# A fused decoder layer on one core: row maxima of two head groups turned over in one tile, the last decision tree finished by halves, and a new planned order

## The chip, the cores and the metric

The kernel runs on one core of a Trainium2 chip. The metric is the device time of one execution in microseconds. Three runs of the kernel before gave 995.1, 996.6 and 993.88 us; their median, 995.1 us, is the time before. In the text, PE is the matrix engine (TensorE), ACT the activation engine (ScalarE), DVE the vector engine (VectorE), POOL is GpSimd, and SP issues the DMAs.

## The reference, cut to what matters

The input is x of shape (2, 1024, 256): 2048 tokens of 256 features, and a context of 2 x 77 rows. Three residual blocks follow each other.

```python
# 1: causal self attention, 16 heads of 16 features, then an iterated cell and a feed-forward layer
xn = ln(x, g_attn, b_attn); q, k, v = split(xn @ qkv_w + qkv_b)
w = softmax(where(causal, -inf, q @ k.T / 4)); attn = (w @ v) @ out_w + out_b
x = x + attn; xs = ln(x, g1, b1); vs = 0
for _ in range(8):
    u = tanh(attn @ w_ctx + xs @ w_x + b_inl)
    vs = vs + 0.1 * (u - xs - vs); xs = xs + 0.1 * vs
x = x + xs; h = ln(x, g2, b2); x = x + gelu(h @ ff_w1 + ff_b1) @ ff_w2 + ff_b2
# 2: cross attention to the 77 context rows, 16 heads, same softmax
# 3: eight decision trees of 255 nodes each
logits = x @ W_in.T + b_in                   # (2048, 8 * 255)
reached = the 8 nodes per tree on the path that the signs of the logits choose
out = (silu(logits) * reached) @ W_out.T
```

Each block's input is first normalised, and its output is added to x.

## The kernel before, in words

The 2048 tokens are cut into NTB = 4 blocks of TB = 512; blocks 0 and 1 are the first sequence, 2 and 3 the second (BPB = 2 blocks a sequence). All arithmetic is fp32 except for small bf16 constants. An fp32 matmul of the program appears in the profile as two PE instructions; a transpose of a 128 x 128 piece as one. The 16 heads lie in NG = 4 groups of 4; a head has a slot of SLOT = 32 partitions, of which the odd ones hold its 16 features and the even ones are free, so the four heads of a group multiply at once on four 32-row strips of the array.

For each block six kinds of stages exist:

- `scores(tb)`: norm, then `queries` (for block 0 `first_queries`): projections of q and k, moved by DMA into the slot layout `qT`, `kT`, values into `v`; then for every group g `maxima(tb, g, q)`: scores with the queries on the partitions, a DVE `tensor_reduce` per head that writes the negated row maximum into the tile `nm`, and `shift`.
- `values(tb)` (`weights` and `weighted`): for each group, once `(tb, g)` is in `done`: scores again with the keys on the partitions, ACT's exponential into `p`, POOL's `affine_select` for the causal mask, the products with `v` (128 x 32 column strips), and `weigh`, which divides by the sum.
- `opening(tb)`, `middle(tb)`: output projection; the cell (`liquid`, eight dependent steps, products with `w_dx`), the feed-forward layer, and `cross_attention`, whose inner function `tops` calls `cross_maxima(xq, k, g)` for the groups one after the other.
- `leaves(tb)` (`trees`): per tree t two halves of 128 nodes: product with the first weights, ACT's bias and halving (`th`), DVE's comparison (`td`), ACT's tanh (`ta`), a DVE product that makes the silu, one product of the signs with the path matrix per half, and a DVE comparison that keeps the reached nodes. The products with the second weights are taken for two trees at a time, for each of DC = 2 output halves `oc` (`outwards`).

How the row maximum gets into the softmax is what the change is about. In `shift(q, nm)` (L814) PE transposes the four 128 x 128 pieces of `nm` into one PSUM bank, and DVE adds the bank to the group's queries. In `nm` only the first column of each slot is written, the others are zero, so after the transpose only partition 0 of each slot carries a value; the keys' partition 0 of each slot is 1 (from `_key_bias`, and the vector `shift`), so the second score product subtracts the maximum by itself. Three tiles `nmax0..2` go round in the list `spare`; each is held from the first reduce of a group to its transposes.

The order on every engine is written out by the program as it builds. `Clock` keeps an account of when each engine is free and each piece of a tile is written and read (`pieces` says at what fineness), with a cost for every operation; `weave` (L380) always takes the next step that can start first by this account, a tie going to the stage whose place in `PLACES` comes first, and `PATIENCE` says for how long a stage is passed over for one that would not make PE wait. So a changed cost, place or patience changes the order of the queues of all engines; what is computed stays. [...]

Of the kernel before, what the change touches and what calls it, by code (L numbers as in the profile page):

```python
# [40 lines left out]
for _name, _k in (  # L41
    ("g_attn", 2), ("b_attn", 2), ("bq", 2), ("bk", 2), ("out_b", 2), ("g1", 2), ("b1", 2),
    ("b_inl", 2), ("g2", 2), ("b2", 2), ("ff_b1", 8), ("xbq", 2), ("xbk", 4),
    ("b_in", 2 * PAR), ("rights", 2), ("shift", 1), ("sbq", 4), ("sbk", 4),
):
    _COLS[_name] = (_n, _k)
    _n += _k
# [12 lines left out]


PLACES = {
    "middle": ((-26, 208), (261, 484), (534, 668), (797, 996)),
    "leaves": ((320, 619), (567, 756), (824, 1044), (1188, 1260)),
    "scores": ((-300, -80), (-51, 138), (138, 375), (464, 619)),
    "opening": ((-24, 87), (181, 344), (399, 404), (656, 885)),
    "values": ((-257, -85), (-141, 85), (251, 381), (434, 634)),
}
PATIENCE = {
    "prepare": 0.5, "projections": 0.3,  # L70
    "middle": 0, "leaves": 0.26, "scores": 0.09, "opening": 0.33, "values": 0,
}


# [32 lines left out]
class Clock:  # L107
# [4 lines left out]
    HANDOVER = 0.06  # L112
    MARGIN = 0.72
    TURNS = {FULL: 0.2, ROWS: 0.215, COLUMNS: 0.135}
    ALONE, MIXED = 1.11, 0.14
    WINDOW, WARM = 3.413, 0.38
    SETS = {AF.Gelu: "gelu", AF.Exp: "exp"}

    def __init__(self, nc):
        self.nc = nc  # L120
        self.pe = 0.0
        self.dma = 2.2
        self.at = {"act": 0.0, "dve": 0.0, "pool": 0.0, "dma": 0.8}
        self.written = {}
        self.used = {}
        self.banks = [0.0] * 8
        self.table = None
        self.mode = (P, P)
        self.each = 0.0
        self.children = []  # L130
        self.window, self.done, self.speed = 0, 0.0, 0.5

    @staticmethod
    def pieces(ap):

        if not hasattr(ap, "ap"):
            ap = ap[:]
        dims = ap.ap
        starts, width = [ap.offset % (dims[0][0] or 1 << 30)], 0
        for step, n in dims[1:]:  # L140
            if step >= P:
                starts = [at + step * i for at in starts for i in range(n)]
            else:
                width += step * (n - 1)
        return {(ap.name, i) for at in starts for i in range(at // P, (at + width) // P + 1)}

    def ready(self, aps):
        return max((self.written.get(p, 0.0) for ap in aps for p in self.pieces(ap)), default=0.0)
# [85 lines left out]
        )  # L234

    def pool(self, name, out, *args, **kw):
        cost = 0.15 + out.free_size() * (0.0009 if name == "affine_select" else 0.0021)
        cost += 0.82 if ALU.pow in args else 0.0

        def issue():  # L240
            if name == "affine_select":
                self.nc.gpsimd.affine_select(out=out, in_=args[0], **kw)  # L242
            else:
                getattr(self.nc.gpsimd, name)(out, *args, **kw)

        return Op("pool", cost, 0.06, out, args, issue)
# [198 lines left out]
def decoder_kernel(ctx: ExitStack, tc: tile.TileContext, ins: dict, out: bass.AP):  # L445
# [19 lines left out]
    def bank():  # L465
        return banks(1)[0]
# [68 lines left out]
    def col(name, i):  # L535
        at = _COLS[name][0] + i
        return vecs[:, at : at + 1]
# [73 lines left out]
    def fill_late():  # L611
        for t in (qT[1], xq, *nmax[2:]):
            yield zeros(t)
        for g in range(NG):
            src = col("shift", 0).to_broadcast([P, S - TB])
# [198 lines left out]
    def shift(q, nm):  # L814


        yield (nm,), 1
        pt = bank()
        for qi in range(NQ):
            clock.transpose(pt[:, qi * P : (qi + 1) * P], nm[:, qi, :], ident)  # L820
        spare.append(nm)
        yield clock.vector("tensor_tensor", q, q, pt, ALU.add)
        clock.free(pt)


# [13 lines left out]
    def queries(tb, xn):  # L839
# [10 lines left out]
            cols = slice(i * P, (i + 1) * P)  # L850
            yield from project_values(v[:, first + i], xn[:, :, cols], wv, vrow[:, 0, :], P, f"v{tb}_{i}")
        done.add((tb, "projected"))
        for g in range(NG):
            yield from maxima(tb, g, q)
            done.add((tb, g))

    def first_queries(xn):

# [10 lines left out]
            done.add((0, "projected"))  # L869

        clock.spawn(others(), PATIENCE["projections"])
        for g in range(NG):
            yield (), lambda: len(made) > g and all(m() for m in made[g])
            yield from maxima(0, g, q)
            done.add((0, g))

    def weights(tb):

# [8 lines left out]
        yield from features_first(aT, at, f"a{tb}")  # L887
        done.add((tb, "aT"))

    def maxima(tb, g, qT):  # L890

        blk = tb % BPB
        yield (), lambda: bool(spare)
        nm = spare.pop(0)
        slots = nm.rearrange("p i (j s) -> p i j s", s=SLOT)[:, :, :, 0]
# [48 lines left out]
        yield from shift(qT[:, g, :], nm)  # L944

    def cross_maxima(xq, k, g):
        yield (), lambda: bool(spare)
        nm = spare.pop(0)
        slots = nm.rearrange("p i (j s) -> p i j s", s=SLOT)[:, :, :, 0]

        def one(j, ps, qi):
            r = slice(j * SLOT, (j + 1) * SLOT)
# [14 lines left out]
        yield from shift(xq[:, g, :], nm)  # L967

    def weighted(tb, g, qT, at):

# [182 lines left out]
    def cross_attention(tb, x):  # L1153
# [4 lines left out]
        ready = []  # L1158

        def tops():  # L1160
            for g in range(NG):
                yield from cross_maxima(xq, k, g)
                ready.append(g)

        clock.spawn(tops())
        at = dtile(f"xat{tb}", (P, NQ, D))
# [41 lines left out]
    def trees(tb):  # L1208
# [12 lines left out]
        def outwards():  # L1221
# [10 lines left out]
            ]  # L1232
            yield (), lambda: all(m() for m in made)
            for t in range(0, PAR, 2):
                yield (), lambda: len(acts) > t + 1
                w2 = [outof[tb * PAR + t + n] for n in range(2)]
                made = []
                for oc in range(DC):
                    for n in range(2):
                        for i in range(2):  # L1240
                            act = acts[t + n][:, i, :]
                            yield (act, w2[n]), 1 if n == i == 0 else None
                            if n == i == 0:
                                ps = bank()
                            clock.matmul(
                                ps, w2[n][:, i, oc * P : (oc + 1) * P], act,
                                start=n == i == 0, stop=n == i == 1,
                            )
                    at = y[:, oc, :]
                    op = clock.vector("tensor_tensor", at, at, ps, ALU.add)  # L1250
                    made.append(clock.beside(added(op, ps, oc, t + 2 == PAR)))
# [7 lines left out]
        for t in range(PAR):  # L1259
# [5 lines left out]
            )  # L1265
            dec = work.tile([P, TB], BF16, tag="dec", name=f"td{tb}_{t}", bufs=2)

            for i in range(2):
                for c in range(DC):
                    yield (xn, w1), 1 if c == 0 else None  # L1270
# [8 lines left out]
                clock.free(ps)  # L1279
                if i == 0:  # L1280
                    yield clock.vector("tensor_scalar", dec, h[:, 0, :], 0.0, None, ALU.is_gt)
            into.more()
            yield clock.activation(act, h, AF.Tanh)
            yield clock.vector("scalar_tensor_tensor", act, act, 1.0, h, ALU.add, ALU.mult)


            for i in range(2):
                yield (dec,), 1
                ps = bank()
                clock.matmul(ps, paths[:, i, :], dec, start=True, stop=True)  # L1290
                yield clock.vector(
                    "scalar_tensor_tensor", act[:, i, :], ps, col("rights", i), act[:, i, :],
                    ALU.is_equal, ALU.mult,
                )
                clock.free(ps)
            acts.append(act)
        yield (), lambda: (tb, "trees") in done


# [121 lines left out]

def _key_bias(v):

    out = _slots(v, 1).reshape(H, SLOT)
    out[:, 0] = 1.0
    return out.reshape(-1)


# [25 lines left out]
def _arrays(a):  # L1454
# [7 lines left out]
    shift = np.tile(np.arange(SLOT) == 0, P // SLOT).astype(np.float32)  # L1462
# [45 lines left out]
```

## Time and profile before

| What | Value |
|---|---|
| runs | 993.88, 995.1, 996.6 us (median 995.1) |
| profiled execution | 993.91 us, its span 992.2 us |
| clock granted to PE | 1.000 of full |
| PE busy | 944.4 us (95%), 6256 matrix instructions |
| DVE busy | 622.3 us (63%), 1357 instructions |
| ACT busy | 411.4 us (41%) |
| POOL busy | 84.6 us (9%) |
| DMA | 44.97 MB, mean 45 GB/s |

A row of a group says: source line, engine, operation, written tile<-read tiles, shapes, count | total busy us, mean ns of one | idle time of that engine just before, and what ended it. The mean ns of a PE instruction is its latency through the pipe; the next one may start earlier, so costs on PE are read here from the distance of starts. `nmax` is the tile `nm` of the code, `bank` any of the eight PSUM banks; L182 is the line that issues every matmul, L198 every transpose, L233 every DVE and L223 every ACT operation.

### The profile page before, as it was taken

What the parts mean: (1) busy time and instruction counts of PE and PEld (TensorE: products, weight loads), DVE (VectorE), ACT (ScalarE), POOL (GpSimd) and SP (SyncE); (2) the same over time, 40 slices, a digit from 0 to 9 for tenths busy, and PEclk for the clock granted to TensorE, in tenths of its full rate; (3) what the DMA queues carried; (4) which work ended last, traced back from release to release, by engine and by line L of the source; (5) the groups of instructions that cost most, each with busy time, mean ns of one, the idle gap of its engine ahead of it and who ended that gap; (6) DMA issues with size and microseconds to landing.
All of it is one profiled execution on the core that took longest, in us unless ns stands there. A gap on an engine that the chain in (4) does not pass through costs nothing. (4 is left out here: it accounts for less than half of the span.)

```text
span 992.2 us, 15604 instructions
## 1 busy us (share of the span) xinstructions
PE 944.4 (95%) x6256; PEld 471.5 (48%) x6256; DVE 622.3 (63%) x1357; ACT 411.4 (41%) x701; POOL 84.6 (9%) x161
## 2 busy tenths in 40 slices
PE   6998999798889999999999989999999999999997
PEld 3654444345436445464544433355455445655443
DVE  4758878854525889637766985827346785355554
ACT  4253444533482534324454342732652333254331
POOL 0121101000110201012002001200000000000000
PEclk9999999999999999999999999999999999999999
DMA  9020001002101011121000001111101021021221
GB/s 333 25 50 16 1 12 33 1 32 75 23 2 44 11 32 44 42 87 46 10 11 12 22 11 44 54 64 64 54 11 43 32 75 64 32 75 33 70 79 42
DMA packets 22568, 44.97 MB, mean 45 GB/s; under 512 B 2912, under 2 KB 3296, under 8 KB 22496
## 3 DMA queue, kind: packets, MB, share of 16 engines
q1 hardware_dynamic: 22496, 43.98, 14.0%
q8 instruction: 49, 0.80, 0.3%
q14 instruction: 23, 0.19, 0.1%
HBM read 36.63 MB, written 2.10 MB: 39 GB/s over the span
## 5 line engine op out<-in xcount | busy, mean ns | idle before, releaser
L223 ACT ACTIVATE p<-bank 128x512 f32<-128x512 f32 (+1 forms) x320 | 154.2, 558 | 128.1 <-PE bank L182 121.0
L233 DVE TENSOR_REDUCE top<-bank 128x1 f32<-128x512 f32 (+3 forms) x256 | 138.9, 580 | 58.7 <-PE bank L182 58.6
L182 PE MATMUL bank<-qT,kT 32*128 32x512 f32 (+3 forms) x768 | 116.6, 522 | 11.2 <-ACT p L223 5.2
L182 PE MATMUL bank<-ta,trees 128*128 128x512 f32 x256 | 124.2, 599 | 1.8 <-DVE ta L233 1.8
L182 PE MATMUL bank<-xn_t,trees 128*128 128x512 f32 x256 | 125.2, 603 | 0.8 <-ACT p L223 0.8
L182 PE MATMUL bank<-kT,qT 32*128 32x512 f32 (+3 forms) x768 | 109.5, 519 | 6.9 <-DVE top L233 3.6
L233 DVE TENSOR_REDUCE nmax<-bank 128x1 f32<-128x128 f32 (+3 forms) x192 | 82.6, 476 | 41.8 <-PE bank L182 40.3
L182 PE MATMUL bank<-w,w_dx 128*128 128x512 f32 x224 | 101.6, 595 | 0.4 <-DVE w L233 0.4
L233 DVE TENSOR_TENSOR x<-x,bank 128x512 f32<-128x512 f32 x48 | 32.8, 684 | 101.1 <-PE bank L182 101.0
L223 ACT ACTIVATE th<-bank,half_b 128x512 f32<-128x512 f32 x64 | 44.1, 689 | 115.7 <-PE bank L182 115.7
L242 POOL TENSOR_SCALAR_AFFINE_SELECT p<-p 128x256 f32<-128x256 f32 x128 | 59.3, 484 | 379.9 <-ACT p L223 189.2
L223 ACT ACTIVATE w<-bank,b_ac 128x512 f32<-128x512 f32 x64 | 44.0, 687 | 85.2 <-PE bank L182 85.2
L182 PEld LDWEIGHTS bank<-xn_t,trees 128*128 128x128 f32 x256 | 45.6, 189 | 54.2 <-issue 45.6
L182 PEld LDWEIGHTS bank<-ta,trees 128*128 128x128 f32 x256 | 47.1, 190 | 51.1 <-issue 42.9
L182 PE MATMUL bank<-p,v 128*32 128x512 f32 (+3 forms) x768 | 70.7, 491 | 0.1
L182 PEld LDWEIGHTS bank<-qT,kT 32*128 32x128 f32 x768 | 43.1, 183 | 48.0 <-ACT p L223 18.4
L182 PEld LDWEIGHTS bank<-w,w_dx 128*128 128x128 f32 x224 | 41.7, 190 | 51.0 <-issue 42.9
L182 PE MATMUL bank<-xn_l,ff 128*128 128x512 f32 x128 | 59.8, 595 | 0.5 <-DVE at L233 0.5
L182 PE MATMUL bank<-ff,ht 128*128 128x256 f32 x256 | 59.4, 379 | 0.0
L182 PEld LDWEIGHTS bank<-ff,ht 128*128 128x128 f32 x256 | 48.6, 190 | 17.6 <-issue 12.2
L233 DVE SCALAR_TENSOR_TENSOR ta<-ta,th 128x1024 f32<-128x1024 f32 x32 | 39.1, 1222 | 26.4 <-ACT ta L223 26.4
L182 PEld LDWEIGHTS bank<-kT,qT 32*128 32x128 f32 x768 | 36.4, 185 | 36.6 <-ACT p L223 12.7
(182 smaller groups left out, 1142.9 us busy)
## 6 DMA issues: line engine op xcount, KB each, us to landing
trees<-in_trees_dram SPq DMA_DIRECT2D x64, 256.0 KB, 2.6
ff<-in_ff_dram SPq DMA_DIRECT2D x32, 256.0 KB, 3.0
xn<-in_xtok_dram SPq DMA_DIRECT2D x4, 512.0 KB, 4.0
kc<-in_xtok_dram SPq DMA_DIRECT2D x4, 512.0 KB, 4.5
x<-in_xtok_dram SPq DMA_DIRECT2D x4, 512.0 KB, 4.1
xq<-xqc SPq DMA_DIRECT2D x16, 128.0 KB, 2.4
out_dram<-x SPq DMA_DIRECT2D x8, 256.0 KB, 2.0
qT<-qc SPq DMA_DIRECT2D x12, 128.0 KB, 2.3
```

The lines of the kernel that those rows point to most:

```text
L182: return self.nc.tensor.matmul(out, w, x, **kw)
L223: lambda: self.nc.scalar.activation(out, x, func, bias=bias, scale=scale),
L233: "dve", cost, 0.085, out, args, lambda: getattr(self.nc.vector, name)(out, *args, **kw)
L242: self.nc.gpsimd.affine_select(out=out, in_=args[0], **kw)
```

## The change

1. Two groups share one tile of maxima. The even group writes column 0 of each slot as before, the odd one column 2 (`slots`: `[:, :, :, g % 2 * 2]`). `shift` is called once for the two: one set of four transposes, and one DVE add of the bank, repeated, to both groups' queries (128 x 1024). The keys of an odd group have their 1 in partition 2 in place of 0 (`_key_bias`, `shift`). Both groups are marked `done` after that one add.
2. In the very last tree (block 3, tree 7) each half goes through tanh, silu, path product and comparison by itself as soon as it is there, and the last pair's second products are ordered tree by tree, so those that need the last tree come last. For all pairs the wait is per half in place of per tree.
3. Some costs of the account change: POOL's select, the extra for two heads issued alone (`ALONE`), the start of the DMA (`self.dma`), and the fineness of pieces for tiles of up to 128 elements a partition.
4. All twenty places and three patiences have other values.

```diff
-    "middle": ((-26, 208), (261, 484), (534, 668), (797, 996)),
-    "leaves": ((320, 619), (567, 756), (824, 1044), (1188, 1260)),
-    "scores": ((-300, -80), (-51, 138), (138, 375), (464, 619)),
-    "opening": ((-24, 87), (181, 344), (399, 404), (656, 885)),
-    "values": ((-257, -85), (-141, 85), (251, 381), (434, 634)),
+    "middle": ((92, 177), (251, 520), (581, 636), (612, 1027)),
+    "leaves": ((279, 578), (515, 713), (937, 1067), (1080, 1119)),
+    "scores": ((-333, -101), (-61, 151), (90, 375), (517, 656)),
+    "opening": ((-38, 36), (184, 295), (298, 303), (616, 879)),
+    "values": ((-165, -138), (-67, 66), (142, 290), (463, 518)),
...
-    "prepare": 0.5, "projections": 0.3,
-    "middle": 0, "leaves": 0.26, "scores": 0.09, "opening": 0.33, "values": 0,
+    "prepare": 0.5, "projections": 0.27,
+    "middle": 0, "leaves": 0.26, "scores": 0.17, "opening": 0.24, "values": 0,
...
-    ALONE, MIXED = 1.11, 0.14
+    ALONE, MIXED = 1.27, 0.14
...
-        self.dma = 2.2
+        self.dma = 1.5
...
+        piece = P if dims[0][0] > P else 2
-            if step >= P:
+            if step >= piece:
...
-        cost = 0.15 + out.free_size() * (0.0009 if name == "affine_select" else 0.0021)
+        cost = 0.15 + out.free_size() * (0.00122 if name == "affine_select" else 0.0021)
...
         spare.append(nm)
-        yield clock.vector("tensor_tensor", q, q, pt, ALU.add)
+        two = pt.rearrange("p (o t) -> p o t", o=1).to_broadcast([P, 2, TB])
+        yield clock.vector("tensor_tensor", q, q, two, ALU.add)
         clock.free(pt)
...
-        for g in range(NG):
-            yield from maxima(tb, g, q)
-            done.add((tb, g))
+        for g in range(0, NG, 2):
+            yield (), lambda: bool(spare)
+            nm = spare.pop(0)
+            yield from maxima(tb, g, q, nm)
+            yield from maxima(tb, g + 1, q, nm)
+            yield from shift(q[:, g : g + 2, :], nm)
+            done.update([(tb, g), (tb, g + 1)])
...
         def tops():
-            for g in range(NG):
-                yield from cross_maxima(xq, k, g)
-                ready.append(g)
+            for g in range(0, NG, 2):
+                yield (), lambda: bool(spare)
+                nm = spare.pop(0)
+                yield from cross_maxima(xq, k, g, nm)
+                yield from cross_maxima(xq, k, g + 1, nm)
+                yield from shift(xq[:, g : g + 2, :], nm)
+                ready.extend([g, g + 1])
...
-                yield (), lambda: len(acts) > t + 1
+                last = t + 2 == PAR
+                yield (), lambda: len(acts) > 2 * t + 2
+                order = [(n, oc) for n in range(2) for oc in range(DC)]
+                if not (last and tb == NTB - 1):
+                    order.sort(key=lambda pair: pair[1])
+                made, pss = [], {}
+                for n, oc in order:
+                    for i in range(2):
+                        yield (), lambda: len(acts) > 2 * (t + n) + i
+                        act, w2 = acts[2 * (t + n) + i], outof[tb * PAR + t + n]
+                        yield (act, w2), None if oc in pss else 1
+                        ps = pss[oc] = pss[oc] if oc in pss else bank()
...
+            def reached(i, before=()):
+                yield (dec,), 1
+                ps = bank()
+                clock.matmul(ps, paths[:, i, :], dec, start=True, stop=True)
+                yield from before
+                yield clock.vector(
+                    "scalar_tensor_tensor", act[:, i, :], ps, col("rights", i), act[:, i, :],
+                    ALU.is_equal, ALU.mult,
+                )
+                clock.free(ps)
+                acts.append(act[:, i, :])
...
+            halves, made = tb == NTB - 1 and t == PAR - 1, []
...
+                if halves:
+                    made.append(clock.beside(reached(i, silu(slice(i, i + 1)))))
             into.more()
-            yield clock.activation(act, h, AF.Tanh)
-            yield clock.vector("scalar_tensor_tensor", act, act, 1.0, h, ALU.add, ALU.mult)
...
+            if halves:
+                yield (), lambda: all(m() for m in made)
+            else:
+                yield from silu(slice(0, 2))
+                for i in range(2):
+                    yield from reached(i)
```

More of the change, by code (lines that the diff above doesn't have):

```diff
@@ L43 @@
     ("b_inl", 2), ("g2", 2), ("b2", 2), ("ff_b1", 8), ("xbq", 2), ("xbk", 4),
-    ("b_in", 2 * PAR), ("rights", 2), ("shift", 1), ("sbq", 4), ("sbk", 4),
+    ("b_in", 2 * PAR), ("rights", 2), ("shift", 2), ("sbq", 4), ("sbk", 4),
 ):
@@ L144, in pieces @@
                 width += step * (n - 1)
-        return {(ap.name, i) for at in starts for i in range(at // P, (at + width) // P + 1)}
+        return {(ap.name, i) for at in starts for i in range(at // piece, (at + width) // piece + 1)}
     def ready(self, aps):
@@ L614, in fill_late @@
         for g in range(NG):
-            src = col("shift", 0).to_broadcast([P, S - TB])
+            src = col("shift", g % 2).to_broadcast([P, S - TB])
             yield clock.activation(kT[:, g, TB:], src, AF.Copy)
@@ L871, in first_queries @@
         clock.spawn(others(), PATIENCE["projections"])
-        for g in range(NG):
-            yield (), lambda: len(made) > g and all(m() for m in made[g])
-            yield from maxima(0, g, q)
-            done.add((0, g))
+        for g in range(0, NG, 2):
+            yield (), lambda: bool(spare)
+            nm = spare.pop(0)
+            for i in (g, g + 1):
+                yield (), lambda: len(made) > i and all(m() for m in made[i])
+                yield from maxima(0, i, q, nm)
+            yield from shift(q[:, g : g + 2, :], nm)
+            done.update([(0, g), (0, g + 1)])
     def weights(tb):
@@ L888, in weights, with maxima @@
         done.add((tb, "aT"))
-    def maxima(tb, g, qT):
+    def maxima(tb, g, qT, nm):
         blk = tb % BPB
-        yield (), lambda: bool(spare)
-        nm = spare.pop(0)
-        slots = nm.rearrange("p i (j s) -> p i j s", s=SLOT)[:, :, :, 0]
+        slots = nm.rearrange("p i (j s) -> p i j s", s=SLOT)[:, :, :, g % 2 * 2]
         tops = work.tile([P, NQ, 4, 2], F32, tag=f"top{tb % 2}", name=f"top{tb}_{g}", bufs=2)
@@ L943, in maxima, with cross_maxima @@
             yield clock.vector("tensor_reduce", slots, tops, AX.X, ALU.min)
[L944 to L949, printed above, removed]
+    def cross_maxima(xq, k, g, nm):
+        slots = nm.rearrange("p i (j s) -> p i j s", s=SLOT)[:, :, :, g % 2 * 2]
         def one(j, ps, qi):
@@ L966, in cross_maxima @@
         yield (), heads.whole
-        yield from shift(xq[:, g, :], nm)
     def weighted(tb, g, qT, at):
@@ L1160, in tops @@
         def tops():
-            for g in range(NG):
-                yield from cross_maxima(xq, k, g)
-                ready.append(g)
+            for g in range(0, NG, 2):
+                yield (), lambda: bool(spare)
+                nm = spare.pop(0)
+                yield from cross_maxima(xq, k, g, nm)
+                yield from cross_maxima(xq, k, g + 1, nm)
+                yield from shift(xq[:, g : g + 2, :], nm)
+                ready.extend([g, g + 1])
         clock.spawn(tops())
@@ L1234, in outwards @@
             for t in range(0, PAR, 2):
-                yield (), lambda: len(acts) > t + 1
[L1236 to L1251, printed above, removed]
+                last = t + 2 == PAR
[10 more added lines that the diff above has]
+                        ps = pss[oc] = pss[oc] if oc in pss else bank()
+                        clock.matmul(
+                            ps, w2[:, i, oc * P : (oc + 1) * P], act,
+                            start=n == i == 0, stop=n == i == 1,
+                        )
+                    if n:
+                        at = y[:, oc, :]
+                        op = clock.vector("tensor_tensor", at, at, ps, ALU.add)
+                        made.append(clock.beside(added(op, ps, oc, last)))
                 step["used"] = t + 2
@@ L1266, in trees, with silu @@
             dec = work.tile([P, TB], BF16, tag="dec", name=f"td{tb}_{t}", bufs=2)
+            def silu(i):
+                yield clock.activation(act[:, i, :], h[:, i, :], AF.Tanh)
+                yield clock.vector(
+                    "scalar_tensor_tensor", act[:, i, :], act[:, i, :], 1.0, h[:, i, :],
+                    ALU.add, ALU.mult,
+                )
+            def reached(i, before=()):
[3 more added lines that the diff above has]
+                yield from before
+                yield clock.vector(
+                    "scalar_tensor_tensor", act[:, i, :], ps, col("rights", i), act[:, i, :],
+                    ALU.is_equal, ALU.mult,
+                )
+                clock.free(ps)
+                acts.append(act[:, i, :])
+            halves, made = tb == NTB - 1 and t == PAR - 1, []
             for i in range(2):
@@ L1281, in trees @@
                     yield clock.vector("tensor_scalar", dec, h[:, 0, :], 0.0, None, ALU.is_gt)
+                if halves:
+                    made.append(clock.beside(reached(i, silu(slice(i, i + 1)))))
             into.more()
-            yield clock.activation(act, h, AF.Tanh)
-            yield clock.vector("scalar_tensor_tensor", act, act, 1.0, h, ALU.add, ALU.mult)
[L1287 to L1296, printed above, removed]
+            if halves:
[4 more added lines that the diff above has]
+                    yield from reached(i)
         yield (), lambda: (tb, "trees") in done
@@ L1422, in _key_bias @@
 def _key_bias(v):
-    out = _slots(v, 1).reshape(H, SLOT)
-    out[:, 0] = 1.0
+    out = _slots(v, 1).reshape(NG // 2, 2, 4, SLOT)
+    for i in range(2):
+        out[:, i, :, 2 * i] = 1.0
     return out.reshape(-1)
@@ L1461, in _arrays @@
     paths, rights = _tree()
-    shift = np.tile(np.arange(SLOT) == 0, P // SLOT).astype(np.float32)
+    shift = np.concatenate(
+        [np.tile(np.arange(SLOT) == 2 * i, P // SLOT).astype(np.float32) for i in range(2)]
+    )
     vectors = {
```

## The prediction, made before the changed kernel was run

> **What bounds the kernel now.** I read the page's busy line first, then its slices, then the chain that ended last, then busy time by windows, and the timeline at the places that the change touches.
>
> ```profile
> span 992.2 us, 15604 instructions
> PE 944.4 (95%) x6256; PEld 471.5 (48%) x6256; DVE 622.3 (63%) x1357; ACT 411.4 (41%) x701; POOL 84.6 (9%) x161
> ...
> PE   6998999798889999999999989999999999999997
> ...
> PE 26%; ACT 1%; DVE 1%; issue 0%; DVEq 0%
> ```
>
> PE is busy for 944.4 of 992.2 us, and the chain consists almost wholly of PE. So an instruction taken from PE shortens the span where PE has no hole beside it, and DVE, ACT and POOL count only where PE waits for them. The 47.8 us in which PE idles are not spread evenly; the windows (columns: stretch, length, PE, PE weight loads, DVE, ACT, POOL) show where they are.
>
> ```profile
> 24.80:124.00 99.20, 92.98 (x1017) 50.24 (x1016) 72.05 (x184) 39.95 (x81) 16.56 (x36) 1.00 0.09 23
> 173.60:297.60 124.00, 108.43 (x978) 52.84 (x978) 65.65 (x153) 62.49 (x119) 13.20 (x27) 1.00 0.09 26
> 446.40:496.00 49.60, 46.30 (x514) 24.14 (x506) 37.52 (x84) 23.66 (x46) 6.50 (x13) 1.00 0.10 28
> 570.40:620.00 49.60, 46.36 (x335) 18.00 (x333) 34.76 (x64) 19.69 (x36) 3.07 (x8) 1.00 0.09 27
> ...
> 297.60:446.40 148.80, 146.99 (x952) 80.33 (x946) 103.53 (x238) 55.39 (x89) 16.07 (x26) 1.00 0.15 43
> 620.00:935.00 315.00, 312.29 (x1584) 161.17 (x1585) 179.59 (x374) 130.66 (x209) 15.50 (x24) 1.00 0.16 52
> 935.00:992.20 57.20, 51.52 (x126) 22.46 (x125) 25.65 (x36) 15.40 (x19) 0.00 (x0) 1.00 0.19 60
> ```
>
> The first four rows, where self attention runs, are thin: PE idles 6.2 + 15.6 + 3.3 + 3.2 = 28.3 us there. In the full stretches between (the two shown and two more) it idles 5.7 us in all. Another 8.2 us lie before 24.8 us, where inputs load, and 5.7 after 935. PE's waits name the cause in the thin stretches: exponentials and maxima that have not yet emptied their banks.
>
> ```profile
> PE bank L182 <- ACT p L223: 18.0, 28, 1.7
> PE bank L182 <- DVE top L233: 8.2, 14, 1.0
> ```
>
> **The change part by part.** *Transposes.* 16 self groups (4 blocks x 4) and 16 cross groups each have a `shift` now; pairs leave 16 of 32.
>
> ```profile
> L198 PE MATMUL bank<-ident,nmax 128*128 128x128 f32 x128 | 19.8, 278 | 0.3 <-DVE nmax L233 0.3
> ```
>
> These 128 instructions become 64. Their mean of 278 ns is latency; the cost is read from starts (columns: start, us, what):
>
> ```profile
> 481.27 0.60 PE L198 MATMUL bank<-ident,nmax 128*128 128x128 f32 x4
> 481.71 0.60 PE L198 MATMUL bank<-ident,raw_x 128*128 128x128 f32 x4
> ...
> 266.60 0.66 PE L198 MATMUL bank<-ident,nmax 128*128 128x128 f32 x4
> 267.18 1.13 PE L182 MATMUL bank<-xk,xq 32*128 32x77 f32 x32
> ```
>
> Between full-size neighbours a shift takes 481.71 - 481.27 = 0.44 us (0.109 each), so 16 x 0.44 = 7.0 us leave PE. Counted by windows with the tile nmax, 18 of the 32 lie in the thin stretches and 14 in the full ones. I count the full share whole, 7 x 0.44 = 3.05 us. The thin share, 9 x 0.44 = 3.95 us, can be worth from nothing (PE would wait for the same exponential anyway) to all; since PE is still busy 87 to 94% there, I take 3.0.
>
> *Mode changes.* A shift uses the whole array; between products on 32-row strips or 32-column strips it is an excursion. The second pair of rows shows one: 267.18 - 266.60 = 0.58 us against 0.44, and the strip product before it also hands over 0.09 us later (0.52 in place of 0.43 from last start to first transpose), so about 0.24 more. [...] The trace says that only 5 of the 32 have strip products on both sides; the others sit next to a full-size product or transpose, where the mode changes anyway. [...]
>
> *The adds.* 32 adds of 128 x 512 become 16 of 128 x 1024 with a repeated operand.
>
> ```profile
> L233 DVE TENSOR_TENSOR xq<-xq,bank 128x512 f32<-128x512 f32 x16 | 10.9, 684 | 15.5 <-PE bank L198 7.7 <-ACT xp L223 5.5 <-ACT p L223 1.9
> L233 DVE TENSOR_TENSOR x<-x,vrow 128x1024 f32<-128x1024 f32 x8 | 9.9, 1241 | 0.0
> ```
>
> The nearest row to the new form is the second, also 1024 long with a repeated operand: 1.24 us. DVE loses 16 x (2 x 0.684 - 1.24) = 2.0 us. It lies beside PE in the full stretches; in the thin ones DVE is one of the two engines waited for. Bounds 0 and 2.0; I take 0.5. Were the repeated read of a bank twice as slow, DVE would gain 16 x 1.24 = 20 us of work over 370 us of slack: bound 2 us of loss.
>
> *The longer hold.* The first group of a pair must wait for the second's maxima. In block 0 this is visible: shifts start at 29.7, 41.0, 63.1 and 80.3, the exponentials' score products of the groups at 41.5, 57.6 and 77.4 for the first three. The first pair costs nothing, since the first scores already wait until 41 for the values. The third group would move from 77.4 past the fourth shift at 80.3: 2.9 us, unless maxima of block 1 fill it. Bounds 0 and 3, I take 1.0. For later blocks the maxima run a block ahead of the weights (`scores` is a thread of its own, queries are double-buffered), so nothing new waits; the three `nm` tiles serve as many threads as before. In cross attention the first exponentials wait for one more maxima unit (32 products of 77 columns, start to start 0.95 us) per block; other blocks' trees or feed-forward cover it. Bounds 0 and 4 x 1 us, I take 0.5. [...] SP's and POOL's queues see the same instructions in another order, none added.
>
> *The last tree.* Here nothing hides anything:
>
> ```profile
> 979.11 0.69 ACT L223 ACTIVATE th<-bank,half_b 128x512 f32<-128x512 f32 x1 [1.89 <-PE bank L182]
> 979.83 1.06 ACT L223 ACTIVATE ta<-th 128x1024 f32<-128x1024 f32 x1
> 980.91 1.23 DVE L233 SCALAR_TENSOR_TENSOR ta<-ta,th 128x1024 f32<-128x1024 f32 x1 [2.64 <-ACT ta L223]
> 982.24 1.41 DVE L233 SCALAR_TENSOR_TENSOR ta<-bank,vecs_sb,ta 128x512 f32<-128x512 f32 x2
> 983.05 5.42 PE L182 MATMUL bank<-ta,trees 128*128 128x512 f32 x12 [1.83 <-DVE ta L233]
> ```
>
> Of the last pair's 16 PE instructions four have run from 979.34, then PE waits 1.83 us, and twelve follow at 0.43 apart until 988.3. After the change the second half's chain is tanh 0.60 (a 128 x 512 ACT row without bias), silu 0.69, comparison 0.74: from 979.83 to about 982.0 with handovers. The eight instructions of the earlier tree last from 979.34 to 982.8, so the last half is ready before PE asks for it. All 16 run through: 979.34 + 16 x 0.43 = 986.2, that is 2.1 us sooner; the last add (0.69) and store follow as now. The price, two ACT and two DVE instructions cut in half, about 0.3 us, is off the path. For the other pairs the finer wait changes nothing on the chip: PE still takes those products in its order.
>
> *The account.* It costs no time itself, it only orders. Three of its numbers come nearer to the trace: POOL's select of 256 elements 0.38 before, 0.46 after, 484 ns measured; the first input's landing, by the old account at 5.8 us, by the new at 5.1, with the first bn_stats at 4.95. Products with `p` waited 7.4 us on the weight-load side for POOL, so that mis-cost bore on real holes.
>
> *The places.* Everything is ordered anew, so every hole of the four thin stretches can move. The trace bounds it: at most 28.3 + 5.7 = 34 us can be won, and an order that is as much worse would lose about as much. With numbers nearer to the chip, and with 7 us less work of the one bounding engine, I take a gain of 3 us, ends -10 and +12.
>
> The sum against the profiled execution: 3.05 + 3.0 + 0.6 + 0.5 + 2.1 - 1.0 - 0.5 = 7.75, and 3 for the order: 10.75. 993.9 - 10.75 = 983.2 us. The median of the runs stands 1.2 us above the profiled execution, so the median to expect is about 984 us.
>
> **The rivals.** *The order wins much more.* Thin stretches are holes of 0.5 to 2.3 us where both evicting engines are late; DVE is busy 53 to 76% in them, ACT 40 to 50%, so neither is full and a better interleaving exists. Half of 28.3 us would give 993.9 - 7.75 - 14 + 1.2 = 973. For it: the 28 waits for `p` last 0.6 us on average, small enough to be filled by another stage. Against: attention and norms have serial chains that no order removes. *The work goes, the wait stays.* The removed transposes become idle time in the thin stretches, the pairs' longer hold costs its full 3 + 4 us, the order gives nothing: 3.05 + 0.6 + 2.1 - 7 is -1.25, so 996; with half of the hold, 992 to 993. *Slower: the last block is left alone.* Block 3's middle stage holds three norms in series with the cell, feed-forward and cross attention between; it is now covered by block 2's trees. If the new places use these trees up early, PE stands through each norm: four statistics at 0.41, aggregates 0.65, POOL's power 1.0, three small DVE steps 0.5, four scalings at 0.41, about 5.4 us. Two exposed norms (10.8) outweigh the 7.75; that is the point from which it decides, and with three the time is 993.9 - 7.75 + 16.2 + 1.2 = 1003.5. For it: block 0's middle goes from place -26 to 92, so the whole chain could end later. Against: block 3's middle begins at 612 in place of 797, and block 2's trees at 937 in place of 824; the filler is kept for the end. *The change does not do what it says:* nothing in the diff could bring the transposes back; the count 64 would show it.
>
> **How the numbers follow.** About 0.3% (3 us) is what a measurement of this kernel can tell from no change. The forecast has 0.62, the much better order 0.15, the wait that stays 0.15, the bare end 0.08. Faster by over 0.3% (under 992.1): the first two and over half of the third, 0.85. Within 0.3% (992.1 to 998.1): most of the rest of the third, 0.07. Slower: 0.08. The forecast alone holds 978 to 990. To leave out no more than 2 in 10 the range reaches into the better order and the staying wait: 974 to 993.
>
> **What would show it.** In the changed profile: 64 transposes of nmax, 16 adds of 128 x 1024 near 1.24 us; PE busy down by some 7 us to about 937; two tanh of 128 x 512 at the end and no hole near 1.8 us before the last products, the distance from the last `th` to the end of the span falling from 13.1 to about 11 us; a first pair in block 0 with its scores still at about 41 us. Idle time of PE in the attention stretches stays between 20 and 34 us. I am wrong in the mechanism if PE busy falls and its idle time rises as much; wrong about the order if idle time before 935 us moves by over 10 us either way; and wrong on the sign if PE shows holes of several us in the last 130 us.

## The result and the profile after

The changed kernel takes 1011.16 us in the median of four runs (1007.0 to 1013.43), the kernel before 995.84 us beside it; the ratio is 1.0152, with a 95% interval of 1.0115 to 1.0189. It is slower by 15 us where 11 us less were forecast, outside the range of 974 to 993.

The page of the changed kernel, its busy line, the slices of PE and of the granted clock:

```profile
span 1009.3 us, 15477 instructions
PE 946.6 (94%) x6192; PEld 465.2 (46%) x6192; DVE 614.6 (61%) x1338; ACT 413.4 (41%) x706; POOL 79.5 (8%) x161
...
PE   6998899889798999999999999899899999999998
...
PEclk9997999999889999999999999999999999999999
```

64 instructions are gone (6192 for 6256), and yet PE is busy for longer, 946.6 for 944.4 us, and idle for 62.7 us in place of 47.8. The row that had no digit below 9 before, PEclk, now has some: over the execution the granted clock is 0.986. PE's waits (total, times, longest):

```profile
PE bank L183 <- ACT p L224: 22.6, 30, 2.6
PE bank L183 <- DVE top L234: 18.9, 25, 1.9
```

They were 18.0 and 8.2. What the diff says is there. The transposes, the adds of both groups, and the last tree:

```profile
L199 PE MATMUL bank<-ident,nmax 128*128 128x128 f32 x64 | 10.0, 279 | 0.0
L234 DVE TENSOR_TENSOR qT<-qT,bank 128x1024 f32<-128x1024 f32 x8 | 9.7, 1216 | 1.3 <-PE bank L199 1.3
...
998.31 0.69 ACT L224 ACTIVATE th<-bank,half_b 128x512 f32<-128x512 f32 x1 [1.89 <-PE bank L183]
998.54 7.03 PE L183 MATMUL bank<-ta,trees 128*128 128x512 f32 x16
998.90 1.14 ACT L224 ACTIVATE ta<-th 128x512 f32<-128x512 f32 x2
999.55 1.29 DVE L234 SCALAR_TENSOR_TENSOR ta<-ta,th 128x512 f32<-128x512 f32 x2 [2.07 <-ACT ta L224]
1000.76 1.40 DVE L234 SCALAR_TENSOR_TENSOR ta<-bank,vecs_sb,ta 128x512 f32<-128x512 f32 x2
```

The add takes 1.22 us (1.24 forecast). All 16 last products run without a hole, and from the last `th` to the end of the span it is now 11.0 us in place of 13.1. So the loss lies ahead of the last tree.

Stretches of the changed kernel in which PE waits most, by windows (PE, PE weight loads, DVE, ACT, POOL, granted clock, DMA):

```profile
75.60:100.80 25.20, 20.66 (x198) 10.07 (x199) 14.97 (x30) 5.94 (x13) 3.07 (x8) 0.80 0.06 21
176.40:226.80 50.40, 40.80 (x465) 16.66 (x463) 35.86 (x82) 24.80 (x48) 8.23 (x17) 0.97 0.01 1
252.00:302.40 50.40, 42.76 (x386) 18.12 (x388) 20.99 (x54) 30.33 (x59) 5.07 (x10) 0.86 0.10 27
604.80:655.20 50.40, 44.50 (x458) 18.02 (x457) 33.19 (x76) 27.61 (x53) 7.17 (x17) 1.00 0.10 31
```

Two things can be read. PE idles 27.7 us in these four; in the same windows of before it was 17.6 (3.8 + 7.1 + 5.3 + 1.4; the fourth is largely full there). And in the first three the clock is cut for part of the time. In finer windows the clock reads 1.00 or 0.50, and a mean of the two where it changes: in this execution it is full or half. The five cuts of this execution begin and end on one grid of 3.41 us; they last 10.24, 3.41, 3.41, 6.83 and 3.41 us. Two of them, each with the stretch of that grid ahead of it:

```profile
84.01:87.42 3.41, 1.84 (x24) 1.03 (x24) 2.48 (x4) 1.61 (x5) 0.82 (x2) 1.00 0.02 5
87.42:97.66 10.24, 8.62 (x56) 2.41 (x48) 4.97 (x8) 2.27 (x7) 2.26 (x6) 0.50 0.00 0
254.68:258.09 3.41, 1.16 (x12) 0.40 (x16) 1.90 (x13) 3.40 (x8) 1.99 (x2) 1.00 0.41 154
258.09:261.50 3.41, 3.41 (x16) 0.53 (x16) 3.08 (x7) 2.71 (x6) 0.00 (x0) 0.50 0.02 5
```

In the first pair PE is busy for a little over half of the stretch, in the second for a third, and what follows runs at half clock. The other three cuts follow stretches in which PE is busy for 1.67, 2.03 and 1.98 of 3.41 us. Two stretches of 1.74 and 1.81 us were followed by none, so busy time alone does not decide it. The timeline shows the price at the second place:

```profile
256.93 1.14 PE L183 MATMUL bank<-qT,kT 32*128 32x512 f32 x8 [2.57 <-ACT p L224]
258.00 3.62 PE L183 MATMUL bank<-p,v 128*32 128x512 f32 x16
261.55 0.71 PE L183 MATMUL bank<-qT,kT 32*128 32x512 f32 x4
```

First PE waits 2.57 us for an exponential; then 16 products with `v` take 3.55 us, from 258.00 to the next start at 261.55; at full clock as many of them take 1.85 us (200.09 to 201.94).

### The profile page after: what moved, and what is told of

It is laid out like the page before. It is cut to its first block, busy times and chain, and to the rows that moved or that the text cites. A ratio compares the mean times of both kernels' runs of the same rounds, so it can differ in the third digit from the quotient of the medians.

```text
span 1009.3 us, 15477 instructions
## 1 busy us (share of the span) xinstructions
PE 946.6 (94%) x6192; PEld 465.2 (46%) x6192; DVE 614.6 (61%) x1338; ACT 413.4 (41%) x706; POOL 79.5 (8%) x161
## 4 chain that ended last, share of the span: by engine, by line
PE 47%; ACT 2%; DVE 1%; issue 0%; ACTq 0%; DVEq 0%
PE bank L183 45%; PE bank L199 2%; DVE top L234 1%; ACT p L224 1%; ACT xp L224 1%; DVE ta L234 0%; ACT ta L224 0%; ACT L224 0%; ACT w L224 0%; DVE w L234 0%; ACT th L224 0%; DVE x L234 0%; ACT raw_x L224 0%; ACT aT L224 0%; DVE td L234 0%
## 5 line engine op out<-in xcount | busy, mean ns | idle before, releaser
L234 DVE TENSOR_REDUCE top<-bank 128x1 f32<-128x512 f32 (+3 forms) x256 | 136.4, 581 | 52.9 <-PE bank L183 52.7
L183 PE MATMUL bank<-qT,kT 32*128 32x512 f32 (+3 forms) x768 | 111.0, 534 | 15.8 <-ACT p L224 8.1
L183 PE MATMUL bank<-kT,qT 32*128 32x512 f32 (+3 forms) x768 | 104.4, 528 | 14.4 <-DVE top L234 10.9
L234 DVE TENSOR_REDUCE nmax<-bank 128x4 f32<-128x308 f32 (+4 forms) x192 | 82.5, 478 | 53.6 <-PE bank L183 53.0
L243 POOL TENSOR_SCALAR_AFFINE_SELECT p<-p 128x256 f32<-128x256 f32 x128 | 54.0, 445 | 449.5 <-ACT p L224 351.1
L183 PE MATMUL bank<-p,v 128*32 128x512 f32 (+3 forms) x768 | 77.3, 530 | 0.2 <-POOL p L243 0.2
L183 PEld LDWEIGHTS bank<-kT,qT 32*128 32x128 f32 x768 | 34.1, 186 | 46.0 <-DVE top L234 23.9
L234 DVE SCALAR_TENSOR_TENSOR ta<-ta,th 128x1024 f32<-128x1024 f32 (+1 forms) x33 | 39.1, 1187 | 24.9 <-ACT ta L224 24.7
```

Of the source, the lines that this page charges most:

```text
L183: return self.nc.tensor.matmul(out, w, x, **kw)
L234: "dve", cost, 0.085, out, args, lambda: getattr(self.nc.vector, name)(out, *args, **kw)
```

## The experiments

Three theories had to be told apart. *Order*: the edits save what they should, but a new order of all queues costs more. *Pairs*: holding two groups together is bad in itself. *Clock*: most of the loss is PE at half clock. The first four kernels take the change apart.

### 1. Pairs and last tree on the old planning numbers; the new numbers alone; the last tree alone; the changed kernel again

```diff
# e1: account, PLACES and PATIENCE as before; shift, maxima, tops and trees as changed
# e2: the other way round
-    "middle": ((-26, 208), (261, 484), (534, 668), (797, 996)),
+    "middle": ((92, 177), (251, 520), (581, 636), (612, 1027)),
...
-    ALONE, MIXED = 1.11, 0.14
+    ALONE, MIXED = 1.27, 0.14
# e3: only the edit of trees (silu, reached, halves, the order of the last pair, the wait per half)
# e4: no edit
```

> The pairs of groups and the halved last tree, with every planning number (account, places, patiences) as before. If the new numbers are what costs 16 us, this order loses its 64 transposes and its end hole without a new loss: 984 to 990 us, clock 1.000. If the pairs themselves cost it, because maxima and exponentials of neighbouring groups can no longer run side by side, it is 1004 us or more, with a granted clock under 0.99 and PE's waits for top and p together over 35 us.

> The kernel before with the new account, places and patiences alone; one transpose set per group, last tree as before. If the new numbers cost the time: 1005 to 1020 us with a clock under 0.99. If the pairs cost it: within 8 us of 995 with a clock of 1.000.

> The kernel before with the last tree by halves alone. The step of the sum: the hole of 1.83 us before the last products goes, 2.1 us less, 993 us. A rival says that the finer wait moves other steps of the order too and the result is anything within 5 us of before.

> The changed kernel again, to have more runs. If the halved clock is the cause of most of the loss, span and granted clock go together over the runs: about 0.5 us of span for each us spent at half clock, so a line through them meets full clock at 993 to 997 us. If the clock only accompanies holes that are there anyway, the span does not follow the clock from run to run.

| kernel | median us | ratio to before, 95% interval | clocks granted |
|---|---|---|---|
| e1 pairs and tree, old numbers | 1020.93 | 1.0251 (1.0217 to 1.0284) | 0.981 to 0.988 |
| e2 new numbers alone | 1027.13 | 1.032 (1.0293 to 1.0347) | 0.978 to 0.985 |
| e3 last tree alone | 1002.29 | 1.0061 (1.0042 to 1.008) | 0.995 to 0.998 |
| e4 changed kernel again | 1007.64 | 1.0126 (1.0104 to 1.0147) | 0.983 to 0.991 |

By its time e1 blames the pairs and e2 the new numbers: both parts alone are slower than both together. (One sign that was named for the pairs is missing in e1: PE's waits for `p` and `top` are 27.4 us there, not over 35.) The old numbers do not fit the pairs, the new numbers do not fit single groups. Even e3, which takes 2 us of waiting from the end and adds no work, is 6 to 7 us slower: its finer wait is one more step in the plan. In the profile its queues of ACT, DVE and POOL are those of before up to 390 us and ordered otherwise from there on. So numbers seem to belong to the program they were found for: each of these three edits made the planner reorder the kernel, at a loss of 6 to 32 us.

e4 gives span and clock of more runs. One program shows clocks from 0.981 to 0.991. With every cut taken to half, as in the profile above, time at half clock is 2 x (1 - clock) x span: 18 to 38 us. A line through the ten runs of the changed kernel rises by 0.35 us of span for each us at half clock and meets full clock (no time at half clock) at 998.7 us. The expectation said 0.5 and 993 to 997: span does follow the clock, with a smaller slope, probably because part of the slowed time is waiting anyway (in the first cut shown above PE is busy for 8.62 of 10.24 us). Before behaves alike, milder: over 46 runs beside the experiments its clock is 0.993 to 1.000 and its span 991.9 to 996.8, slope 0.33, full clock at 992.3. So 6.4 of the 15 us remain at full clock, with less work, and the other half and a little more goes with the clock. The profiles separate the two as well: in the profiled execution of e4, at a clock of 0.991, PE is busy for 941.1 us and idle for 63.3; in the one above, at 0.986, it was 946.6 and 62.7. The cuts show as busy time. The idle time, some 15 us more than the 47.8 of before, is there with fewer cuts too.

### 2. The edits with the order kept, the clock held up, and the account alone

```diff
# e5: kernel before; the last tree by halves, with every step ahead of it planned as before
+            halves, waits = tb == NTB - 1 and t == PAR - 1, []
...
+                if halves:
+                    waits.append(clock.beside(half(i)))
...
# e6: kernel before; transposes of odd groups accounted for but not issued
     def transpose(self, out, x, ident, leave_out=False):
         self.array(0.109, (P, P), out, x)
+        if leave_out:
+            return None
...
+        if g % 2:
+            op.issue = lambda: nc.vector.tensor_tensor(q, q, q, ALU.max)
# e7: changed kernel; products that only keep PE active, outside the account
         heads = [(unit, j, *unit.banks(1)) for unit, j in heads]
+        self.units += 1
+        if self.units in WARM_UP:
+            w, x = self.idle
+            for _ in range(2):
+                self.nc.tensor.matmul(heads[0][2], w, x, start=True, stop=True)
# e8: kernel before; only the account's lines of the diff
```

> The kernel before with the last tree by halves, written so that no step ahead of it is planned otherwise: PE's queue is the old one up to its last products. Theory (the work removed counts, the new order ate it): the hole of 1.83 us goes and the span falls by 2.1 us, to about 990 at full clock. Rival (the step of the sum was wrong): no gain, 992.

e5 takes 993.68 us, ratio 0.9975 (0.9963 to 0.9987), its profiled span 989.9. The end of its timeline:

```profile
978.89 0.69 ACT L223 ACTIVATE th<-bank,half_b 128x512 f32<-128x512 f32 x1 [1.89 <-PE bank L182]
...
979.12 7.03 PE L182 MATMUL bank<-ta,trees 128*128 128x512 f32 x16
```

From `th` to the end of the span it is 11.0 us as in the changed kernel, and here nothing was lost ahead of it. This step of the sum was right to a few tenths, and it alone makes a kernel faster than both.

> The kernel before, order of all queues kept, where the odd groups' 64 transposes are not issued and their add is one of the same length on the queries alone (the odd groups' softmax goes without its maximum: this part is left out). It is an upper bound for what the pairs can save without a new order. My sum says 6 to 7.5 us (3.05 sure, up to 3.95 in the thin stretches, 0.6 for modes): a span of 985 to 986 at full clock. If PE only waits longer in the thin stretches: 3 us, 989. If less work lets the clock fall: a granted clock under 0.995 and a span of 992 or more.

e6 takes 991.97 us, ratio 0.9952 (0.994 to 0.9965): 4.6 us less by medians. A line through its six runs meets full clock at 988.3, so 4.0 us below that of before, where 6 to 7.5 were expected. PE busy fell by 5.8 us (938.6), its waits for p and top rose:

```profile
PE 938.6 (95%) x6181; PEld 465.1 (47%) x6192; DVE 622.1 (63%) x1357; ACT 411.4 (42%) x701; POOL 84.8 (9%) x161
...
PE bank L182 <- ACT p L225: 18.5, 28, 1.7
PE bank L182 <- DVE top L235: 8.7, 14, 1.0
```

They were 18.0 and 8.2, so 1 us of what was removed came back as these two waits. As an upper bound (no odd group waits for its maxima here) the transposes that pairs save are worth about 4 us without a new order, not 7; the shorter adds are no part of this test. One profiled execution cannot settle where the rest went; it has a dip of the clock of its own, to 0.99 in the windows from 173 to 297 us.

> The changed kernel with two bf16 products of the full array (0.22 us each) ahead of 33 of the strip units that PE waits for in the first 310 us, written to a bank that the unit itself overwrites afterwards; order and results as in the changed kernel. If the halved clock comes from too little PE activity in those holes and costs 6 to 12 us: clock back to 0.996 or more and a span of 998 to 1000. If the clock falls for another reason, it stays at 0.98 to 0.99 and the extra products cost up to 14 us more: 1010 to 1020.

e7 takes 1001.29 us, ratio 1.0049 (1.0029 to 1.0069), though it does 66 products more than the changed kernel. Its clock is 0.991 to 1.000 (profiled 0.996), and at full clock it is at 997.6. The windows of the first three thin stretches, to be held against those of the changed kernel above:

```profile
75.60:100.80 25.20, 22.90 (x253) 11.25 (x254) 18.74 (x40) 8.36 (x18) 3.60 (x10) 1.00 0.02 7
176.40:226.80 50.40, 45.46 (x470) 19.86 (x469) 33.07 (x76) 23.26 (x45) 7.34 (x17) 1.00 0.02 7
252.00:302.40 50.40, 46.94 (x464) 19.54 (x468) 17.79 (x37) 33.68 (x69) 6.12 (x16) 0.97 0.06 12
```

The clock goes from 0.80, 0.97 and 0.86 to 1.00, 1.00 and 0.97. The order is the same (in the profile the queues of all engines are those of the changed kernel but for the added products), and these sit in holes that PE had anyway, since they wait only for the first of the unit's banks to come free. With more PE work there, and nothing else changed, the clock stays up: that ties the cuts to the thin stretches, at a price of 6 to 10 us (1001.3 against 1007.6 and 1011.2). Some of it is left: the third stretch still reads 0.97, and the lowest run 0.991. What in an added product does it, its time or its use of the whole array, is not separated here.

> The kernel before with the new account alone (select, two heads alone, start of DMA, finer pieces), the same work, places and patiences. If numbers nearer to the chip's durations make better orders by themselves: 985 to 995. If the old places fit only the old account, the order is merely another one: 998 to 1015.

e8 takes 1012.5 us, ratio 1.0156 (1.014 to 1.0171), with a clock of 0.988. With the same work and the same places, corrected costs alone lose 16 us. That three of the new numbers lie nearer to the trace was no reason to expect a better order. The account's own sum, the time at which it has PE end, stands beside the chip: 978.2 us for before, 969.3 for the changed kernel, 998.2, 998.6 and 985.8 for e1, e2 and e3, 976.3 for e5 and 983.0 for e8. Kernels planned with the old costs take 16 to 23 us more than this on the chip, those planned with the new costs 28 to 42. So the account did foresee a loss of 20, 20 and 8 us for e1, e2 and e3; for the changed kernel it promised 9 us of gain.

### 3. Two versions that follow from these

```diff
# e9: e5, and two keeping products ahead of 21 units that PE waits for in the trace of before
+WARM_UP = {128, 130, 149, 150, 27, 30, 52, 54, 55, 57, ...}
# e10: pairs, and the last tree as in e5, on the account of before, with places and patiences searched anew
-    "middle": ((-26, 208), (261, 484), (534, 668), (797, 996)),
+    "middle": ((-20, 112), (223, 491), (629, 797), (854, 1000)),
...
```

> The kernel of the kept order with the last tree by halves, with two bf16 products of the full array ahead of 21 strip units that PE waits for in the trace of before. If the low-activity holes are what lets the clock fall in some runs of this order too: clock 1.000 in every run, span 989 to 990.5 without the spread of 4.7 us, a median near 991. If the products come in the way: 992 to 996.

> The pairs and the last tree by halves on the account of before, with places and patiences found by a search that was charged for stretches of 3.4 us in which PE would be active under about half. If the pairs are sound and the changed kernel's order and clock are its loss: 990 to 1000 and a clock of 0.996 or more. If pairs are bad for every order: 1005 or more, with the waits for p and top over 35 us.

e9 takes 991.61 us, ratio 0.9963 (0.995 to 0.9977), the fastest of all; its six runs lie within 0.25 us (991.56 to 991.81) with a clock of 0.999 or 1.000, where e5 spread from 991.6 to 996.4. The page and PE's wait:

```profile
PE 954.2 (96%) x6298; PEld 474.1 (48%) x6298; DVE 622.4 (63%) x1358; ACT 411.2 (42%) x702; POOL 84.4 (9%) x161
...
PE   6998999999999999999999999999999999999998
...
PEclk9999999999999999999999999999999999999999
...
PE bank L186 <- ACT p L227: 11.0, 26, 1.2
```

PE is busy 10 us longer than before, and the kernel is faster and steadier: the wait for p fell from 18.0 to 11.0 because the products fill it. Between the fourth slice and the last no slice of PE is below 9 here; in before five were, and its thinnest stretch on the clock's grid of 3.41 us had PE busy for 1.70 us. The gain over e5 lies in its slower runs, as the fastest of e5 took 991.6 us too; the kernel before, run beside e9, still spread from 993.7 to 998.5.

e10 takes 996.39 us, ratio 1.0017 (0.9998 to 1.0037), with clocks from 0.988 to 1.000; at full clock its line stands at 991.8. The expected clock of 0.996 or more came in seven of its twelve runs. It has the same pairs as e1, which took 1020.93, so pairs are not bad in themselves: at full clock this order is level with before (992.3), though not at the 986 that the saved work would allow. The 25 us between e1 and e10 are not the places alone, for e10 has the last tree in the form of e5, and between e3 and e5 this form alone makes 9 us. That no order of pairs was found that beats e9 leaves open whether one exists.

## Why the prediction was wrong

*The places, +3 us of gain: this step failed.* Kept-order runs say what the edits are worth: 2.5 us for the tree and at most 4 for the transposes, so about 986 us at full clock. The changed kernel's line stands at 998.7. The order therefore costs some 13 us at full clock (a little less, as the 4 us are an upper bound; and whatever the longer hold costs is in it), which is at the loss end of my bounds (-10 and +12) or past it; I had taken 3 us of gain. The sign that I had named for a wrong order came: PE's idle time before 935 us rose by 15.7 us, from 42.2 to 57.9. The error was to argue from a quality of the new numbers (nearer to the trace, searched). By the program's own sum, which a search can minimise, the changed order ends 9 us earlier than the old one; that is arithmetic and no chip time, and the chip does not follow it. e8 shows on the chip that a truer cost is not a better order, e3 that an edit of no work costs 6 us. Why the account is most wrong for the changed order stays open. I had also said that a worse order could lose about the 34 us of idle time, and then allowed a loss of 10 to 12; e2 lost 32 us with the old work. And the chain that I called almost wholly PE adds up to 28% of the span: it reaches back to about 714 us and says nothing of the thin stretches, where the loss came.

*The clock: not in the prediction at all.* I read a PEclk row of nines and a clock of 1.000 in one profiled execution and gave the clock no term. Before's other runs go down to 0.993, and the kernel's own account has a term for PE at half speed (in `array`), which I passed over. The longest wait of PE for p in the changed kernel is 2.6 us, and four of the five cuts in its profile come behind stretches with no gap over 1 us, so a search for long gaps would not have found them. Busy time does not name them either: they follow stretches of 3.41 us in which PE is busy, by the profile, which counts each product's latency, for 1.16, 1.67, 1.84, 1.98 and 2.03 us, and those of 1.74 and 1.81 us were followed by none. What decides between them was not shown. This term was worth 6 to 10 us (e7).

*Transposes, 6.05 us, and modes, 0.6 us.* The count (64) and the cost of each (0.109 between full-size neighbours) were right; the sum was mis-sized. No run shows the 0.6 us for modes by itself: the trace of before shows single excursions (0.24 us for one), and e6 bounds both terms together by about 4 us. Of the thin share, where bounds were 0 and 3.95, the value 3.0 was too near the upper one.

*The adds* were right in size (1.22 us against 1.24): 16 of them now take 19.5 us where 32 took 21.8. No relief for PE is seen from it: its waits for `top` rose from 8.2 to 18.9 in the new order.

*The longer hold* went nearly as drawn for block 0: the second pair's transposes run at 77.7 us and the third group's exponentials follow, their score products at 81.3 us in place of 77.4 (3.9 us later, 2.9 drawn). Whether holding costs more elsewhere is not separated. Around 204 us mixed units of two maxima and two exponentials follow each other with the banks not free in time:

```profile
203.86 0.70 PE L183 MATMUL bank<-kT,qT 32*128 32x512 f32 x2 [0.78 <-DVE top L234]
...
205.78 0.70 PE L183 MATMUL bank<-kT,qT 32*128 32x512 f32 x2 [0.78 <-DVE top L234]
...
207.73 0.70 PE L183 MATMUL bank<-kT,qT 32*128 32x512 f32 x2 [0.81 <-DVE top L234]
```

Every unit of 1.93 us has a hole of 0.8 in which PE waits for a maximum. That e10 has pairs without losing time argues that such runs of holes belong to the order, not to the pairs; it was not shown unit by unit.

*The last tree* was right: 2.1 us forecast, 2.3 from span to span at nearly equal clock (989.9 at 0.999 from 992.2 at 1.000). *The rivals*: the slower one I had named, block 3's norms bare at the end, did not happen; the slices of after show 9 in PE from 732 us up to the last one. The slower side came from the thin stretches that I had down as "the work goes, the wait stays", with a chance of 0.15 and a price that stopped at zero gain.

Still open: which of the account's four corrections does the harm of e8, and what exactly decides that the clock is cut. The same order shows clocks from 0.981 to 0.991 in its ten runs; why they differ was not shown.

## What to carry to other kernels

In a kernel whose queue order comes out of a planner, an edit has two prices: its work, and a new order; only a run with the order kept separates them, and the second can be the larger. A bounding engine at 95% says little about stretches at 81 to 85%: there, work taken off PE can come back as waiting (in e6, 1 of the 5.8 us did), and behind some of the thinnest stretches here, with PE busy for 1.16 to 2.03 of 3.41 us, its clock was cut as well. Look at the clock of several runs, not of one; where it dips, a few products that nobody needs, put into holes that wait for a bank anyway, can be worth more (6 to 10 us in e7) than the work that an edit saves (about 4 us in e6).

## What the hardware did that I had not expected

In the profiled execution of the changed kernel the granted clock fell to half for one to three steps of 3.41 us at a time. Ahead of one such cut PE had a gap of 2.57 us, ahead of the others only a few of 0.6 to 0.9 us. Adding 66 unneeded products made the changed kernel 6 to 10 us faster, and adding 42 to the best one took its spread from 4.8 us (twelve runs) to 0.25 us (six). The profile counts such a slowed stretch as PE busy, so PE's busy time rose by 2.2 us while 64 instructions were removed; with fewer cuts (e4's profile) it is 3.3 us below that of before.
